# A pre-norm decoder layer: the wide row blocks of three Gram matrices from 12-bit parts

## The chip, the core and the metric

The kernel runs on one core of a Trainium2 chip. The core has five engines with a queue of instructions each: TensorE (PE, matrix multiplication; its weight loads are listed apart as PEld), VectorE (DVE), ScalarE (ACT), GpSimd (POOL) and SyncE (SP, which only issues transfers here). Engines work through their own queues in order and wait for one another through semaphores. The metric is the time of one execution on the device, in microseconds (us); lower is better.

## The reference, cut to what matters

One decoder layer, batch 4, sequence length T = 512, model width D = 512, all in float32: attention, cross-attention and a feed-forward part, each behind a layer norm and added to x.

```python
def attn(x, ...):                       # 16 heads of 128; x is layer-normed
    q = (x @ Wq + bq).reshape(4, 512, 128, 16).transpose(0, 3, 2, 1)   # 128 x T
    k = (x @ Wk + bk).reshape(4, 512, 128, 16).transpose(0, 3, 1, 2)   # T x 128
    v = (x @ Wv + bv).reshape(4, 512, 128, 16).transpose(0, 3, 2, 1)
    att = softmax(q @ k / sqrt(128))    # 128 x 128: over channels, not positions
    return concat_heads(att @ v) @ Wo + bo
x = x + attn(layernorm(x))
x = x + gamma * cross(layernorm(x), ctx, ctx)   # q, k, v cut into 8 heads of 64 x 512
x = x + (silu(h @ w1q.T) * (h @ w3q.T)) @ w2q.T # h = layernorm(x); HID = 1365
```

w1q, w3q and w2q are the ternary-quantised weights, w + (q - w) with q = clip(round(w / s), -1, 1) * s and s the mean of |w|.

The scores of a head are a contraction over the T rows: q k = Wq' (xn' xn) Wk, with xn the normed rows and the bias carried by a column of ones. So xn' xn, a matrix of 512 x 512 called the Gram matrix, serves all heads of a batch. It is symmetric.

## The kernel before

**Stages.** The first batch's attention comes first, with the weights prepared beside it. Then a loop over b = 1 to 3 (L977) does the attention of the second, third and fourth batch, and inside it, as side steps, the cross-attention of the batch before and the quantisation of w1, w3 and w2. The feed-forward part of all batches follows (L1069 on), with the last batch's cross-attention in it.

**Parts.** Most products of attention are not made in float32. A tensor is held as three tiles, h, l and d (class `Tri`; `tri_of`, L187): h is the source times H_OF, rounded to the 12 bits that a one-pass matmul takes (type fp32r), l the source less h, and d = h / S - l, with S = 4096. `products` (L329) sums h h + l l over four row groups in one PSUM bank (L336, L337), copies it to SBUF on ScalarE (L343), sums d d in another bank (L348), and `total` (L358) joins the two on VectorE with the factor 1 + 1/S on the first. A product is then 12 matmuls of one pass for 4 in float32. The parts of the weights lie in DRAM and are loaded again for every batch by SP's queue into an 18-buffer pool; for `o` in the second batch h and l alone are loaded and VectorE makes d (L322, from ol, a tile of ones and oh) in `weights`.

**The Gram matrix** is `gram_upper` (L422). xn lies in SBUF as four tiles xs[g] of 128 rows (on the partitions) x 512 columns. For row block m (0 to 3) only the columns from m * 128 on are made, so the blocks are 512, 384, 256 and 128 wide, each a sum of four float32 matmuls, evicted by ScalarE into G[m] (L420). In the second to fourth batch the order is m = 0, 1, 2, 3; after m = 1, `midway` transposes on TensorE (bank pe, copied to eT by ScalarE) the softmax e of the last group of heads of the batch before. `output` (L548, bank po) then applies that softmax and adds into the four tiles acc on VectorE. `gram_rest` (L451) fills the lower blocks by transposes of upper ones (bank gt, L458) and splits G[0] to G[3] into parts gh, gl, gd.

**The groups of heads.** For each batch and each of four groups of four heads (j): `values_out` (banks pu: x parts by Wo parts, giving u and its parts), `keys_of` (py: G parts by Wk parts, giving y), `output` of the group before, `values_of` (pm: Wv parts by u parts, giving m), and `scores` (bank sc, float32: q by y, then the softmax). x3, the parts of xn, is made by `parts_of`: at the end of the first batch for the second one, and in the last group of a batch for the next, ahead of `values_of`.

**Order.** Each engine runs its instructions in the order in which a scheduler of the compiler put them; that order is fixed when the kernel is built. The side steps are handed out by `tick`, a fixed number per piece of a product. Among them are the row norms of the batch before (`row_norms`: mv_c on VectorE, two transfers through DRAM that GpSimd issues, norm_a and norms, L673 and L676, and then settle on norms, L596), the inputs of cross-attention (qs, kh, kl: L707 to L716), its scores (bank xs, L726 and L727) and its output (bank xo, L770). GpSimd issues the side steps' transfers, the loads of x into acc and the load of the bias bo; its few computations before are casts in the feed-forward part (L138).

**Pools** that the change touches: u3p (12 buffers, parts of u), yp (5, where G and y lie), tp (3, the SBUF copies of PSUM banks).

Of the kernel before, what the change touches and what calls it, by code (L numbers as in the profile page):

```python
# [19 lines left out]
P = 128  # L20
# [19 lines left out]
def decoder_layer_kernel(  # L40
# [25 lines left out]
    def bank(name):  # L66
        return psum.tile([P, 512], F32, tag="bank", name=name)
# [147 lines left out]
    def exact(n, b, j):  # L215
        return b > 0 or j >= FIRST[n]
# [202 lines left out]
    def evict(dst, src):  # L419
        nc.scalar.copy(dst, src)  # L420

    def gram_upper(b, xs, midway=None):  # L422
        pool, tag = (x3p, "x3") if b == 0 else (yp, "y")
        G = [pool.tile([P, D], F32, tag=tag, name=f"G_{b}_{m}") for m in range(KC)]
        pg = {}

        def add(m, g):
            if g == 0:
                pg[m] = bank(f"pg_{b}_{m}")
            nc.tensor.matmul(  # L430
                pg[m][:, : D - m * P],
                lhsT=xs[g][:, ts(m, P)],
                rhs=xs[g][:, m * P :],
                start=(g == 0),
                stop=(g == NG - 1),
            )
            if g == NG - 1:
                evict(G[m][:, m * P :], pg[m][:, : D - m * P])


        if b == 0:
            order = [(m, g) for g in range(NG) for m in range(KC)]
        else:
            order = [(m, g) for m in range(KC) for g in range(NG)]
        for m, g in order:
            add(m, g)
            if midway and (m, g) == (1, NG - 1):
                midway()
        return G

    def gram_rest(b, G):  # L451

# [40 lines left out]
    def values_of(b, j, w, u3, tick):  # L493
        ms = {}

        def done(g, h, d):
            ms[g] = mp.tile([P, D], F32, tag="m", name=f"m_{b}_{j}_{g}")
            total(ms[g], h, d)

        products(f"pm_{b}_{j}", lambda k, g: cols(w[k], g), lambda k: u3[k], done, tick)  # L500
        return ms

    def scores(b, j, w, ys):

        scale = (S if exact("k", b, j) else 1.0) / math.sqrt(DH)
        sc = bank(f"sc_{b}_{j}")
        for g in range(NG):
            for k in range(KC):
                nc.tensor.matmul(  # L509
                    sc[:, ts(g, DH)],  # L510
                    lhsT=w[k][:, ts(g, DH)],
                    rhs=ys[k][:, ts(g, DH)],
                    start=(k == 0),
                    stop=(k == KC - 1),
                )
        nmax = small.tile([P, NG], F32, tag="nmax", name=f"nmax_{b}_{j}")
        mark["nmax"] = nc.vector.reduce_max(
            nmax, sc.rearrange("p (h k) -> p h k", h=NG), axis=AX.X
        ).ins
        nc.vector.tensor_scalar(nmax, nmax, -scale, None, ALU.mult)  # L520
        e = ep.tile([P, GW], F32, name="e")
        den = small.tile([P, NG], F32, tag="den", name=f"den_{b}_{j}")
        for g in range(NG):
            nc.scalar.activation(
                e[:, ts(g, DH)],
                sc[:, ts(g, DH)],
                AF.Exp,
                bias=nmax[:, g : g + 1],
                scale=scale,
                accum_out=den[:, g : g + 1],  # L530
            )
        rden = small.tile([P, NG], F32, tag="rden", name=f"rden_{b}_{j}")
        nc.vector.reciprocal(rden, den)
        for g in range(NG):
            nc.vector.tensor_scalar(
                e[:, ts(g, DH)], e[:, ts(g, DH)], rden[:, g : g + 1], None, ALU.mult
            )
        return e
# [326 lines left out]
    for j in range(HG):  # L865
        us, ys, ms = {}, {}, {}

        def to(tiles, pool, tag, name):
            def done(i, p, d=None):
                tiles[i] = pool.tile([P, 512], F32, tag=tag, name=f"{name}_{i}")  # L870
                if d is None:
                    evict(tiles[i], p)
                else:
                    total(tiles[i], p, d)

            return done

        ticks = [0]

        def third_tick():  # L880
            ticks[0] += 1
            if ticks[0] == 3:
                midway()

        def midway():
            if waiting:
                waiting[2] = turned(*waiting[:3])

        w = first_weights("o", j, first, gates["o"])
        if exact("o", 0, j):  # L890
            w = keep_weights("o", j, w, first, gates["o"])
            products(
                f"pu_0_{j}", lambda c, m: cols(x3[c], m), lambda c: w[c],
                to(us, u3p, "u3", f"u_0_{j}"), lambda: None,
            )
        else:
            products_f32(
                f"pu_0_{j}", lambda c: xs[c], lambda c: w[c], to(us, u3p, "u3", f"u_0_{j}")
            )
            if j == 0:  # L900
                g3 = gram_rest(0, G)
            with tc.issue_after(rows_done):
                keep_weights("o", j, w, first, gates["o"])
        gates["v"] = gate_of(us[3])
        if j == 1:
            biased(accs, bo_bc)
        w = first_weights("k", j, first, gates["k"])
        done = to(ys, yp, "y", f"y_0_{j}")
        if exact("k", 0, j):
            w = keep_weights("k", j, w, first, gates["k"])  # L910
            products(
                f"py_0_{j}", lambda e, m: cols(g3[e], m), lambda e: w[e], done, third_tick
            )
        else:
            products_f32(f"py_0_{j}", lambda e: G[e], lambda e: w[e], done, midway)
            keep_weights("k", j, w, first, gates["k"])
        gates["o"] = gates["k"] = gates["q"] = gate_of(ys[3])
        if waiting:
            output(*waiting)
        w = first_weights("v", j, first, gates["v"])  # L920
        products_f32(f"pm_0_{j}", lambda k: w[k], lambda k: us[k], to(ms, mp, "m", f"m_0_{j}"))
        keep_weights("v", j, w, first, gates["v"])
        w = first_weights("q", j, first, gates["q"])
        if j == HG - 1:
            normed(1, xs, False)
        e = scores(0, j, w, ys)
        keep_weights("q", j, w, first, gates["q"])
        if j == 0:
            bo_bc = bias_rows(0)
            load(gam, gamma.to_broadcast([P, 1]))  # L930
        if j + 1 == FIRST["o"]:
            x3 = parts_of(0, xs)
        if j == HG - 2:
            xs = rows_of(1)
        if j == HG - 1:

            with tc.issue_after(mark["nmax"]):
                x3 = parts_of(1, xs)
        waiting = [0, j, e, ms, accs]
    first_pools.close()  # L940

    inputs_f = {}
# [34 lines left out]
    for b in range(1, B):  # L977
        def midway():
            waiting[2] = turned(*waiting[:3])

        G = gram_upper(b, xs, midway)
        recent[:] = [G[0], G[0]]
        output(*waiting)
        side = Side(
            itertools.chain(row_norms(b - 1, waiting[4]), cross(b - 1, *cpool)),
            NORM_STEPS + CROSS_STEPS,
            TICKS + 6,
        )

        def tick():  # L990
            quant.tick()
            side.tick()

        bo_bc = bias_rows(b)
        g3 = gram_rest(b, G)
        for j in range(HG):
            u3 = values_out(b, j, x3, weights("o", b, j, wp), tick)
            if j > 0:
                waiting[2] = turned(*waiting[:3])
            ys = keys_of(b, j, g3, weights("k", b, j, wp), tick)  # L1000
            if j > 0:
                output(*waiting)
            else:
                accs = accumulators(b, bo_bc)
            if j == HG - 2:
                xs = rows_of(b + 1)
            if j == HG - 1 and b + 1 < B:
                normed(b + 1, xs, False)
                x3 = parts_of(b + 1, xs)
            elif j == HG - 1:  # L1010
                for t in xs:
                    settle(t)
                ffn_0 = prepare_ffn(0, xs)
                for _ in range(NC):
                    next(ffn_0)
            ms = values_of(b, j, weights("v", b, j, wp), u3, tick)
            e = scores(b, j, weights("q", b, j, wp), ys)
            if j == 0:
                biased(accs, bo_bc)
            waiting = [b, j, e, ms, accs]  # L1020
        side.rest()
# [155 lines left out]
```

## Time and profile before

| | us |
|---|---|
| median of 3 runs | 1152.76 (1149.95 to 1154.46) |
| profiled execution, span | 1150.0 |
| TensorE busy | 1140.7 |
| VectorE busy | 818.7 |
| ScalarE busy | 523.5 |
| GpSimd busy | 295.9 |
| third batch: Gram matrix, first matmul to output | 409.21 to 418.39 |

How to read it: the span is the time from the first to the last instruction of one execution; the profiled execution is a single one and stands 2.8 us below the median of the timed runs. Busy times overlap, since engines work side by side. In rows of a timeline the columns are start (us), duration (us), engine, line, operation, out<-in by the program's names, tile shapes and the number of instructions that the row puts together; an idle time before it and what ended it stand in brackets. The mean of the granted TensorE clock is 0.999 of full speed. The DMA engines moved 235 GB/s in the mean, and were busy for 0.8 and more of the time in most slices of the first 800 us.

### The profile page before, as it was taken

How to read it: one execution, taken by the hardware profiler on the slowest of the kernel's cores; microseconds unless marked ns; L12 is line 12 of the kernel's file. 1: busy time of each engine (PE TensorE's matmuls, PEld its weight loads, DVE VectorE, ACT ScalarE, POOL GpSimd, SP SyncE). 2: the span in 40 equal slices, each digit the busy share in tenths (PEclk: the TensorE clock that was granted, in tenths of full speed). 3: DMA queues.
4: the chain of work that ended last, by engine and by line, in shares of the span. 5: the costliest groups of instructions: out<-in, count | busy, mean ns of one | idle time of the engine just before them, and what ended most of it. 6: DMA issues, size and time to landing. Idle time of an engine off the chain costs nothing.

```text
span 1150.0 us, 16662 instructions
## 1 busy us (share of the span) xinstructions
PE 1140.7 (99%) x5310; PEld 858.6 (75%) x5310; DVE 818.7 (71%) x1818; ACT 523.5 (46%) x1071; POOL 295.9 (26%) x534
## 2 busy tenths in 40 slices
PE   9999999999999999999999999999999999999998
PEld 5486585787778767877776787777778877777886
DVE  6857766978788965969696769788857856536242
ACT  4534334354535442644354445445355768534020
POOL 3435433433133232213221422122113212000000
PEclk9999999999999999999999999999999999999999
DMA  9999996998889769988986798799791422122100
GB/s 332 306 344 337 345 314 225 324 319 280 281 281 308 261 201 325 312 272 276 321 291 215 256 334 271 254 330 325 268 304 40 122 79 65 48 73 72 64 1 37
DMA packets 146177, 270.68 MB, mean 235 GB/s; under 512 B 18276, under 2 KB 49300, under 8 KB 146090
## 3 DMA queue, kind: packets, MB, share of 16 engines
q1 hardware_dynamic: 112218, 164.93, 43.4%
q0 software_dynamic: 33872, 104.70, 26.8%
q8 instruction: 42, 0.69, 0.2%
q14 instruction: 45, 0.37, 0.1%
HBM read 206.62 MB, written 62.93 MB: 234 GB/s over the span
## 4 chain that ended last, share of the span: by engine, by line
PE 96%; DMA 2%; DVE 1%; issue 1%; ACT 0%; POOL 0%; SPq 0%; DVEq 0%; POOLq 0%; ACTq 0%
PE h L1084 13%; PE y L1119 7%; PE xo L770 5%; PE xp L126 5%; PE po L548 5%; PE pm L370 5%; PE sc L509 5%; PE pg L430 3%; PE xs L727 3%; PE xs L726 2%; PE pu_2h L336 1%; PE pu_1d L348 1%; PE py_3h L336 1%; PE py_3h L337 1%; PE pu_2h L337 1%; PE py_2h L337 1%
## 5 line engine op out<-in xcount | busy, mean ns | idle before, releaser
L1084 PE MATMUL h<-fxh,t 128*128 128x512 f32 (+1 forms) x352 | 139.6, 397 | 0.0
L1084 PE MATMUL h<-fxl,t 128*128 128x512 f32 (+1 forms) x352 | 137.4, 390 | 0.0
L737 ACT ACTIVATE p<-xs,xnmax 128x512 f32<-128x512 f32 x128 | 87.2, 689 | 84.8 <-PE xp L126 68.2
L731 DVE TENSOR_REDUCE xnmax<-xs 128x1 f32<-128x512 f32 x128 | 83.5, 684 | 19.3 <-PE xs L727 19.3
L1084 PEld LDWEIGHTS h<-fxh,t 128*128 128x128 f32 (+1 forms) x352 | 65.0, 185 | 15.4 <-issue 1.1
L1084 PEld LDWEIGHTS h<-fxl,t 128*128 128x128 f32 (+1 forms) x352 | 65.0, 185 | 14.7 <-issue 0.2
L1119 PE MATMUL y<-t,gh 128*128 128x512 f32 (+1 forms) x176 | 69.3, 394 | 0.0
L1119 PE MATMUL y<-t,gl 128*128 128x512 f32 (+1 forms) x176 | 68.8, 391 | 0.0
L129 ACT COPY pt<-xp 128x512 f32<-128x512 f32 x96 | 54.1, 595 | 31.0 <-PE xp L126 31.0
L126 PE MATMUL xp<-ident,p 128*128 128x128 f32 x512 | 66.5, 273 | 0.0
L126 PEld LDWEIGHTS xp<-ident,p 128*128 128x128 f32 x512 | 59.3, 140 | 9.4 <-issue 2.4
L770 PE MATMUL xo<-pt,vals 128*64 128x512 f32 x256 | 61.5, 599 | 0.0
L1097 DVE SCALAR_TENSOR_TENSOR gf<-h,scales_w,sl 128x512 f32<-128x512 f32 (+1 forms) x44 | 32.9, 747 | 39.8 <-PE h L1084 36.4
L749 DVE TENSOR_SCALAR p<-p,xrden 128x512 f32<-128x512 f32 x128 | 56.7, 486 | 2.9
L548 PE MATMUL po<-m,eT 128*128 128x512 f32 x128 | 57.6, 593 | 0.0
L1093 ACT ACTIVATE sl<-h,scales_w 128x512 f32<-128x512 f32 (+1 forms) x44 | 30.1, 688 | 58.7 <-PE h L1084 58.5
L689 POOL DMA_DIRECT2D xd<-x_a x64 | 33.8, 532 | 88.6 <-DVE qs L710 64.5
L370 PE MATMUL pm<-u,v_raw 128*128 128x512 f32 x128 | 55.6, 592 | 0.0
L727 PE MATMUL xs<-kl,qs 128*128 128x512 f32 x128 | 50.1, 391 | 0.5 <-DVE kl L714 0.5
L138 POOL CAST gh<-gf 128x512 fp32r<-128x512 f32 (+1 forms) x24 | 15.8, 660 | 134.9 <-DVE gf L1097 119.7
L726 PE MATMUL xs<-kh,qs 128*128 128x512 f32 x128 | 50.1, 392 | 0.0
L139 DVE TENSOR_TENSOR gl<-gf,gh 128x512 fp32r<-128x512 f32 (+1 forms) x44 | 30.4, 690 | 26.3 <-POOL gh L138 19.3
(313 smaller groups left out, 2897.6 us busy)
## 6 DMA issues: line engine op xcount, KB each, us to landing
oh<-kept_oh SPq DMA_DIRECT2D x48, 256.0 KB, 5.9
ol<-kept_ol SPq DMA_DIRECT2D x48, 256.0 KB, 6.2
kh<-kept_kh SPq DMA_DIRECT2D x48, 256.0 KB, 5.2
kl<-kept_kl SPq DMA_DIRECT2D x48, 256.0 KB, 5.9
vh<-kept_vh SPq DMA_DIRECT2D x48, 256.0 KB, 6.6
vl<-kept_vl SPq DMA_DIRECT2D x48, 256.0 KB, 6.9
q<-kept_q SPq DMA_DIRECT2D x48, 256.0 KB, 6.6
od<-kept_od SPq DMA_DIRECT2D x44, 256.0 KB, 6.8
```

Of the source, the lines that this page charges most:

```text
L126: nc.tensor.transpose(pt[:, ts(k, P)], src[:, ts(k, P)], ident)
L370: nc.tensor.matmul(p, lhsT=lhs(k)[:, ts(i, P)], rhs=rhs(k), start=(k == 0), stop=(k == 3))
L509: nc.tensor.matmul(sc[:, ts(g, DH)], lhsT=w[k][:, ts(g, DH)], rhs=ys[k][:, ts(g, DH)], start=(k == 0), stop=(k == KC - 1),)
L548: nc.tensor.matmul(po, lhsT=eT[:, g, :], rhs=ms[g], start=True, stop=True)
L726: nc.tensor.matmul(sc, lhsT=q[:, ts(m, P)], rhs=kh, start=True, stop=False)
L727: nc.tensor.matmul(sc, lhsT=q[:, ts(m, P)], rhs=kl, start=False, stop=True)
L731: nc.vector.reduce_max(nmax[:, i : i + 1], scs[i], axis=AX.X)
L737: nc.scalar.activation(p, scs[i], AF.Exp, bias=nmax[:, i : i + 1], scale=xscale, accum_out=den[:, i : i + 1],)
L749: nc.vector.tensor_scalar(ps[i], ps[i], rden[:, i : i + 1], None, ALU.mult)
L770: nc.tensor.matmul(po[half, :], lhsT=vals[c][:, l, half], rhs=pt[j][:, l, :], start=(l == 0), stop=(l == NC - 1),)
L1084: nc.tensor.matmul(ph[:r, :], lhsT=t[:, block(i, k)], rhs=fxT[j][:, k, :], start=(k == 0 and j == 0), stop=(k == KC - 1 and j == 1),)
L1119: nc.tensor.matmul(py, lhsT=g[i][j][:r, ts(c, P)], rhs=t2[:r, i, :], start=(i == 0 and j == 0), stop=(i == NHC - 1 and j == 1),)
```

## The change

For the second to fourth batch `gram_upper` makes the narrow blocks (m = 2 and 3) first, in float32 as before, with the factor 1/S at the eviction. The wide blocks (m = 0 and 1) are made from the parts x3 that the batch's pu products use anyway: h by a scaled copy of h (h / S, the new tiles xs_b_g) and l by l into banks pgh, then `midway`, two copies on ScalarE (tiles pgt), d by d into banks pgd, and on VectorE G = (1 + 1/S) * pgt - pgd. So the whole of G is 1/S of what it was; `scores` multiplies its scale by S in these batches. `scaled_rows` makes the four scaled tiles on GpSimd, in buffers of u3p: behind the first batch's loop for the second batch, and in the last group of heads, between `values_of` and `scores`, for the next one. The first batch is as before. In the changed kernel later lines move down: the softmax's po from L548 to L586, for instance, xs from L726 and L727 to L764 and L765; the scaling is L485, the new matmuls L457, L460 and L472, the copies L467 and the joining L475.

```diff
--- before.py
+++ after.py
@@ -419,7 +419,7 @@
     def evict(dst, src):
         nc.scalar.copy(dst, src)
 
-    def gram_upper(b, xs, midway=None):
+    def gram_upper(b, xs, midway=None, x3=None, scaled=None):
         pool, tag = (x3p, "x3") if b == 0 else (yp, "y")
         G = [pool.tile([P, D], F32, tag=tag, name=f"G_{b}_{m}") for m in range(KC)]
         pg = {}
@@ -435,18 +435,56 @@
                 stop=(g == NG - 1),
             )
             if g == NG - 1:
-                evict(G[m][:, m * P :], pg[m][:, : D - m * P])
+                if b == 0:
+                    evict(G[m][:, m * P :], pg[m][:, : D - m * P])
+                else:
+                    nc.scalar.mul(G[m][:, m * P :], pg[m][:, : D - m * P], 1.0 / S)
 
 
         if b == 0:
-            order = [(m, g) for g in range(NG) for m in range(KC)]
-        else:
-            order = [(m, g) for m in range(KC) for g in range(NG)]
-        for m, g in order:
-            add(m, g)
-            if midway and (m, g) == (1, NG - 1):
-                midway()
+            for g in range(NG):
+                for m in range(KC):
+                    add(m, g)
+            return G
+        for m in range(2, KC):
+            for g in range(NG):
+                add(m, g)
+        upper = (0, 1)
+        ph = {m: bank(f"pgh_{b}_{m}")[:, : D - m * P] for m in upper}
+        for m in upper:
+            for g in range(NG):
+                a, c = x3[g], slice(m * P, D)
+                nc.tensor.matmul(
+                    ph[m], lhsT=a.h[:, ts(m, P)], rhs=scaled[g][:, c], start=(g == 0), stop=False
+                )
+                nc.tensor.matmul(
+                    ph[m], lhsT=a.l[:, ts(m, P)], rhs=a.l[:, c], start=False, stop=(g == NG - 1)
+                )
+        midway()
+        hs = {}
+        for m in upper:
+            hs[m] = tp.tile([P, 512], F32, tag="t", name=f"pgt_{b}_{m}")[:, : D - m * P]
+            nc.scalar.copy(hs[m], ph[m])
+        for m in upper:
+            pd = bank(f"pgd_{b}_{m}")[:, : D - m * P]
+            for g in range(NG):
+                a = x3[g]
+                nc.tensor.matmul(
+                    pd, lhsT=a.d[:, ts(m, P)], rhs=a.d[:, m * P :], start=(g == 0), stop=(g == NG - 1)
+                )
+            nc.vector.scalar_tensor_tensor(
+                G[m][:, m * P :], hs[m], 1.0 + 1.0 / S, pd, ALU.mult, ALU.subtract
+            )
         return G
+
+    def scaled_rows(b, x3):
+
+        tiles = []
+        for g in range(NG):
+            t = u3p.tile([P, D], F32R, tag="u3", name=f"xs_{b}_{g}")
+            nc.gpsimd.tensor_scalar(t, x3[g].h.bitcast(F32), 1.0 / S, None, ALU.mult)
+            tiles.append(t)
+        return tiles
 
     def gram_rest(b, G):
 
@@ -502,7 +540,7 @@
 
     def scores(b, j, w, ys):
 
-        scale = (S if exact("k", b, j) else 1.0) / math.sqrt(DH)
+        scale = (S if exact("k", b, j) else 1.0) * (S if b > 0 else 1.0) / math.sqrt(DH)
         sc = bank(f"sc_{b}_{j}")
         for g in range(NG):
             for k in range(KC):
@@ -937,6 +975,7 @@
             with tc.issue_after(mark["nmax"]):
                 x3 = parts_of(1, xs)
         waiting = [0, j, e, ms, accs]
+    scaled = scaled_rows(1, x3)
     first_pools.close()
 
     inputs_f = {}
@@ -978,7 +1017,7 @@
         def midway():
             waiting[2] = turned(*waiting[:3])
 
-        G = gram_upper(b, xs, midway)
+        G = gram_upper(b, xs, midway, x3, scaled)
         recent[:] = [G[0], G[0]]
         output(*waiting)
         side = Side(
@@ -1014,6 +1053,8 @@
                 for _ in range(NC):
                     next(ffn_0)
             ms = values_of(b, j, weights("v", b, j, wp), u3, tick)
+            if j == HG - 1 and b + 1 < B:
+                scaled = scaled_rows(b + 1, x3)
             e = scores(b, j, weights("q", b, j, wp), ys)
             if j == 0:
                 biased(accs, bo_bc)
```

## The prediction, made before the changed kernel ran

> **What bounds the kernel now.** I read the page's engine shares and its chain of waits first, then the timelines of TensorE and of its weight loads around a Gram matrix, then VectorE and GpSimd at the same places.
>
> ```profile
> PE 1140.7 (99%) x5310; PEld 858.6 (75%) x5310; DVE 818.7 (71%) x1818; ACT 523.5 (46%) x1071; POOL 295.9 (26%) x534
> ...
> PE 96%; DMA 2%; DVE 1%; issue 1%; ACT 0%; POOL 0%; SPq 0%; DVEq 0%; POOLq 0%; ACTq 0%
> ```
>
> TensorE (PE) has work in 99% of the span and the chain runs through it for 96%. So TensorE time that goes is gained, and each wait that appears on TensorE is lost; all else counts only through such a wait. Third batch, TensorE's Gram matrix, then sixteen one-pass matmuls of py (first and next row):
>
> ```profile
> 409.21 6.28 PE L430 MATMUL pg<-xn 128*128 128x512 f32 x16
> 415.33 0.60 PE L126 MATMUL pe<-ident,e 128*128 128x128 f32 x4
> 415.77 2.78 PE L430 MATMUL pg<-xn 128*128 128x256 f32 x16
> 418.39 3.60 PE L548 MATMUL po<-m,eT 128*128 128x512 f32 x8
> ...
> 409.75 0.19 PEld L430 LDWEIGHTS pg<-xn 128*128 128x128 f32 x1 [0.24 <-issue]
> 410.18 0.19 PEld L430 LDWEIGHTS pg<-xn 128*128 128x128 f32 x1 [0.24 <-issue]
> ...
> 433.42 0.39 PE L336 MATMUL py_0h<-kh,gh 128*128 128x512 f32 x1
> ...
> 437.07 1.19 PE L348 MATMUL py_0d<-kd,gd 128*128 128x512 f32 x4
> ```
>
> Durations overlap, so starts count. A float32 matmul is two records 0.43 us apart (410.18 - 409.75): 0.86 us for 512 columns. A one-pass matmul of 512 columns takes (437.07 - 433.42) / 16 = 0.228. The wide blocks hold TensorE for 415.33 - 409.21 = 6.12 us, 3.43 of it for 512 columns, so 2.69 for 384; the narrow ones for 418.39 - 415.77 = 2.62.
>
> **The matmuls.** In each of three batches 8 wide float32 matmuls (6.12 us) give way to 24 one-pass ones. The 12 of 512 columns cost 12 x 0.228 = 2.74. No row has one of 384 columns: not under half a record of that width (2.69 / 8 / 2 = 0.168), not over 0.228. I take 0.228 x 0.336 / 0.43 = 0.178, by the ratio of the float32 rows: 2.14. So 6.12 - 4.88 = 1.24 us saved per batch (0.6 to 1.4), 3.7 in all. The narrow blocks are the same matmuls, placed first.
>
> **ScalarE.** Two copies out of PSUM go (0.59 and 0.48 us) and two of the same sizes come (L467); the narrow evictions get a factor. Nothing is added, but the copies of the wide blocks end later.
>
> **VectorE, second batch.** Two results per batch are added (L475): 0.69 us as for od below, and some 0.53 for 384 columns. What matters is what stands behind them: L475 needs the last d matmul, and this queue keeps its order. Before, od, made from ol and oh in this batch only, stood between the x parts and po:
>
> ```profile
> 195.57 0.68 DVE L189 TENSOR_TENSOR xl<-xn,xh 128x512 fp32r<-128x512 f32 x1
> ...
> 199.31 1.41 DVE L322 SCALAR_TENSOR_TENSOR od<-ol,one,oh 128x512 fp32r<-128x512 f32 x2
> ...
> 204.47 0.75 DVE L322 SCALAR_TENSOR_TENSOR od<-ol,one,oh 128x512 fp32r<-128x512 f32 x1
> ...
> 206.91 1.98 PE L348 MATMUL pu_0d<-od,xd 128*128 128x512 f32 x8
> ```
>
> VectorE has no gap from 195.57 on; od was complete at 205.2, 1.7 us before TensorE used it. In the built order of the changed kernel the four od stand behind both L475, four acc and all eight gl and gd. From the end of G_0's last d matmul: 0.25 us until VectorE starts, 0.6 + 0.5 for L475, 4 x 0.65 for acc, 8 x 0.605 (their spacing in a row) for gl and gd, 0.1 for two small ones, 0.5 of waiting for gh_2 (two evictions and two gh behind gt): od_0 starts after 9.4 and ends after 10.2. TensorE from the same moment: the last matmul of G_1 0.17, po 3.43, gt 0.4, sixteen pu_0h 3.64, two more gt 0.2: it wants od_0 after 7.9. It waits 2.3 us; the next od follow 0.66 apart, as fast as TensorE takes them. Later in this stage the 0.87 us that pm_0d waited for vd shrinks, since transfers go on meanwhile: I credit 0.4. Net 1.9 lost (0 if VectorE and ScalarE catch up, 2.5 without the credit).
>
> **GpSimd.** Twelve multiplications of 128x512 are new. The nearest rows are its casts, 0.62 us alone, and this one:
>
> ```profile
> 964.22 0.75 DVE L710 SCALAR_TENSOR_TENSOR qs<-xd,norms,qs 64x512 fp32r<-64x512 f32 x1
> ...
> 964.32 1.13 POOL L138 CAST gh<-gf 128x512 fp32r<-128x512 f32 x1 [7.28 <-DVE gf L1097]
> ```
>
> Beside a VectorE operation that reads two tensors from SBUF the cast ended only 0.48 us after that one: 0.5 longer. [...] By the row second-batch Gram comes out even, by a wait to the end of the run 2.7 us longer, as in the second case below.
>
> In the third and fourth batch the x parts are made some 8 us before Gram needs them (last xd at 401.32, Gram at 409.21 and its narrow part first), so 4 x 1.13 = 4.5 us is hidden; without that cover it would all be a stall. In the second batch nothing covers it. xs_1 to xs_3 stand in GpSimd's queue behind loads that waited until 190.54 for the scores and ended at 192.17, and xs_2 needs xh_2, which ScalarE finished at 195.05. With 1.13 each: xs_1 at 193.3, xs_2 at 196.2, xs_3 at 197.4. TensorE starts at 190.08, is through the narrow blocks at 192.70 and the first two row groups at 194.5, waits for the softmax (VectorE, 195.0) and for xs_2, and ends at 199.2, against 199.16 before. So here the 1.24 saved is eaten by idling: 0 (-0.3 with multiplications of 0.62).
>
> **Queues.** SP's order does not change. GpSimd's loads of acc wait for st_c, which VectorE now does behind gd; that moves about 1 MB later. norm_a and norms also move, see the third case. The changed softmax scale costs nothing.
>
> **Sum.** Second batch 0 + 1.9 = +1.9; third and fourth -1.24 each; +0.6 as half of the 1.2 us by which VectorE, held up by GpSimd at 397 to 403, may hand pt late to xo in the third batch. That is 0.0: span 1150.0, as before. The runs' median is 1152.76, 2.8 over the profiled span, so 1152.8, and I say 1153. Own range of this case: 1150 to 1156.
>
> **The rivals.**
>
> 1. *Full gain.* No stall in the second batch: -3.7, 1149. For it: VectorE's order is all that delays od. Against it: both queues are written down and the sum above misses by 2 us. Chance 0.12.
>
> 2. *GpSimd held to the end of a run of VectorE operations.* xs_2 starts at 195.1, but xl_2, xd_2, xl_3 and xd_3 follow without a gap until 198.1, so it ends at 198.55, xs_3 at 199.2; with 3.1 us of matmuls behind xs_2, po starts at 201.75 and not 199.16: +2.6. With od +1.9, the other batches -2.5 and pt late in full, 1.2: +3.2, 1156. For it: the cast above made next to no progress beside qs. Against: no row shows two such operations in a row beside GpSimd. Chance 0.20.
>
> 3. *The row norms come late (the other side).* Third batch, before:
>
> ```profile
> 432.17 0.55 POOL L673 DMA_DIRECT2D norm_a<-mv_c  x1 [0.34 <-DVE mv_c L672]
> ...
> 439.67 1.40 POOL L676 DMA_DIRECT2D norms<-norm_a  x2 [5.01 <-DMA norm_a<-mv_c]
> ...
> 445.08 0.16 DVE L596 TENSOR_TENSOR norms<-norms,one 128x1 f32<-128x1 f32 x1
> ```
>
> mv_c to norms took 13.2 us through two transfers, at a DMA share of 0.99. Now mv_c's copy stands behind y_0_0 and y_0_1, which ended at 441.85: some 440.9 with TensorE 1.2 earlier, so norms at 454.1. VectorE and ScalarE stand still at it; qs, kh, two m and kl follow until 458.1. TensorE's first xs, at 462.4 before, comes at 461.1: 3 us to spare, 8 before. In the fourth batch norms at 664.39 becomes 670, kl 674, xs 677: 3 us again. If each of the transfers takes 3 us longer than before, 6 - 3 = 3 us are lost per batch, 6 in all: 1159. It decides once mv_c to norms exceeds 16 us. Against: acc's loads, moved later, leave room for the weights just before. Chance 0.26.
>
> That the change doesn't do what it says is left 0.01: with h, l and d as built, (1 + 1/S)(h h/S + l l) - d d is G/S, and the softmax multiplies by S.
>
> **How the numbers follow.** The first reading has 0.41. Half a per cent is 5.8 us, about what a measurement of this kernel can tell from no change. Faster by that needs more than the whole saving: 0.07, for the full gain with the waits for kd (1.04 us) and vd (0.87) gone too, which makes 3.7 + 1.9 = 5.6, and something more. Slower by that is most of the third rival and the tail of the second: 0.25. Within: 0.68. The range reaches from the full gain, 1148.5, to the third rival with transfers that take 3.5 us longer each instead of 3, which adds 2: 1161.
>
> **What would show it.** In the profile of the changed kernel: 24 one-pass matmuls of L457, L460 and L472 per batch, 4.9 us without a gap in the third and fourth; TensorE idle before L457 in the second, released by POOL; idle before pu_0d there, released by DVE od L322, about 2 us; L485 at 0.62 to 1.13 us, and longer beside runs of VectorE if the second rival holds; mv_c to norms, and idle before L764 xs, for the third. I am wrong if od isn't waited for, if the 384-column matmuls cost as much as those of 512, or if a wait far from Gram carries the difference.

## The result and the profile after

The changed kernel takes 1159.70 us in the median of four runs (1158.46 to 1160.71), the kernel before 1152.44 (1149.95 to 1154.46). The ratio, taken over all executions, is 1.0067, with a 95% interval of 1.0051 to 1.0083: slower by 5.9 to 9.6 us, 7.7 by the ratio itself. Below, a difference that stands beside a ratio is that ratio's and not that of the two medians. The profiled execution has a span of 1158.9 us against 1150.0.

The engine shares and the chain of waits of the changed kernel, the two lines that were read first before:

```profile
PE 1142.9 (99%) x5334; PEld 865.1 (75%) x5334; DVE 823.5 (71%) x1824; ACT 523.8 (45%) x1071; POOL 315.6 (27%) x546
...
PE 87%; DMA 5%; DVE 4%; issue 2%; ACT 1%; POOL 1%; SPq 0%; DVEq 0%; POOLq 0%; ACTq 0%
```

TensorE's share of the chain fell from 96% to 87%; transfers now hold 5% of it and VectorE 4%. TensorE's busy time did not fall by the 3.7 us that were forecast, but rose by 2.2: the three Gram matrices have 2.6 us of work less, one stretch at half speed (below) has 3.5 more, and smaller pieces add 1.3, 0.7 of it ahead of the second batch. The other 6.7 of the 8.9 us that the span grew are waits. The list of TensorE's waits (us in total, times, longest):

```profile
PE py_0d L348 <- DMA kd<-kept_kd: 3.3, 3, 1.3
PE pu_1d L348 <- DMA od<-kept_od: 2.3, 4, 1.1
PE pu_0d L348 <- DVE od L322: 1.7, 1, 1.7
PE pgh L457 <- POOL xs L485: 1.4, 2, 1.0
```

The first was 1.0 before and the second 0.7; the last two are new. Lining up TensorE's matmuls of the two profiled executions, one by one, gives where the 8.9 us arise (the shift of the changed kernel against the one before at the end of each stretch, and by how much it changed in that stretch; beside it what the prediction had there):

| stretch | shift at its end | measured | predicted |
|---|---|---|---|
| up to the second batch's Gram matrix | 0.41 | +0.41 | 0 |
| that Gram matrix, to po | 1.36 | +0.95 | 0 |
| po to pu_0d | 3.22 | +1.86 | +2.3 |
| to the third Gram matrix | 3.68 | +0.46 | +0.2 (-0.4 for vd, +0.6 for pt) |
| third Gram matrix | 2.54 | -1.14 | -1.24 |
| to the fourth | 3.17 | +0.63 | 0 |
| fourth Gram matrix | 2.25 | -0.92 | -1.24 |
| first py of the fourth batch | 9.05 | +6.80 | 0 |
| the rest | 8.93 | -0.12 | 0 |

The +0.63 on the way to the fourth Gram matrix is what is left of two larger changes: the waits for kd that the kernel before has at 438 to 440 us are spared (the shift falls from 2.4 to 0.8), and new waits for od bring it to 3.1.

The one-pass matmuls do what was said of them. Third batch, TensorE's timeline:

```profile
412.89 2.88 PE L430 MATMUL pg<-xn 128*128 128x256 f32 x16
415.53 0.47 PE L457 MATMUL pgh<-xs,xh 128*128 128x512 f32 x1
...
418.87 0.60 PE L126 MATMUL pe<-ident,e 128*128 128x128 f32 x4
419.22 1.87 PE L472 MATMUL pgd<-xd 128*128 128x512 f32 x8
420.93 3.60 PE L586 MATMUL po<-m,eT 128*128 128x512 f32 x8
```

The 24 take 418.87 - 415.53 = 3.34 and 420.93 - 419.22 = 1.71, so 5.05 us for the 6.12 of the float32 ones (4.88 were forecast). The whole Gram matrix with its transposes takes 8.04 us; it was 9.18.

Most of the loss is in a place that holds no changed instruction, the first py of the fourth batch:

```profile
658.30 0.61 PE L348 MATMUL py_0d<-kd,gd 128*128 128x512 f32 x2
660.25 0.73 PE L348 MATMUL py_0d<-kd,gd 128*128 128x512 f32 x2 [1.34 <-DMA kd<-kept_kd]
662.12 1.22 PE L348 MATMUL py_0d<-kd,gd 128*128 128x512 f32 x2 [1.13 <-DMA kd<-kept_kd]
664.17 1.22 PE L348 MATMUL py_0d<-kd,gd 128*128 128x512 f32 x2 [0.82 <-DMA kd<-kept_kd]
665.19 0.63 PE L336 MATMUL py_0h<-kh,gh 128*128 128x512 f32 x1
```

TensorE waits three times for kd, 3.3 us in all. And look at the last line: a one-pass matmul of 512 columns, 0.39 us long in most rows of this record, is 0.63 long; the next starts 0.43 behind it and not 0.228. The busy time by stretches says why (the column behind POOL is the granted clock, then the share of the transfer engines and GB/s):

```profile
660.00:662.00 2.00, 0.73 (x2) 0.30 (x2) 0.46 (x1) 0.77 (x2) 0.00 (x0) 1.00 1.04 383
662.00:664.00 2.00, 1.22 (x2) 0.50 (x2) 0.00 (x0) 0.00 (x0) 0.00 (x0) 0.50 1.05 391
664.00:666.00 2.00, 1.83 (x4) 1.49 (x5) 1.00 (x2) 0.00 (x0) 0.00 (x0) 0.50 0.93 341
666.00:668.00 2.00, 2.00 (x6) 1.57 (x5) 1.21 (x6) 0.00 (x0) 1.04 (x2) 0.50 0.40 94
668.00:670.00 2.00, 2.00 (x8) 1.59 (x8) 0.00 (x0) 0.00 (x0) 0.04 (x1) 0.79 1.00 355
```

From 662.0 to 668.8 TensorE is granted half its clock. That costs half of 6.8, 3.4 us, and with the waits 6.7 of the 6.8 in the table. It is no accident of the execution that was profiled: the mean granted clock of the four was 0.996, 0.997, 0.997 and 0.997, and 0.003 of 1150 us is 3.5; the kernel before stands at 0.999 to 1.000.

Why kd is late, by the list of transfers issued between 640 and 665 us (size, then the median time from issue to landing):

```profile
acc<-in_x_dram POOLq DMA_DIRECT2D x4, 256.0 KB, 6.8
kd<-kept_kd SPq DMA_DIRECT2D x4, 256.0 KB, 10.1
```

and by the same list for the kernel before, between 638 and 663:

```profile
acc<-in_x_dram POOLq DMA_DIRECT2D x4, 256.0 KB, 4.9
kd<-kept_kd SPq DMA_DIRECT2D x4, 256.0 KB, 6.2
```

SP issues kd just as early against TensorE as before (7.6 us behind the start of pu_0h in both, 651.01 - 643.43 and 648.76 - 641.18), but it takes 3.9 us longer to land. In the five microseconds behind 645.3 the transfer engines move 130 GB/s, at a share of 0.40; at the same point of the kernel before it was 252, at 0.78. GpSimd issued the four loads of acc at 643.1 to 647.7 before, ahead of kd. Now they leave at 650.4 to 659.4, in among kd and vh, since each waits for the st_c (the statistics of the row norms) that reads its buffer, and VectorE has those behind gd. The first and the last of the four, before:

```profile
643.08 0.54 POOL L849 DMA_DIRECT2D acc<-in_x_dram  x1 [0.52 <-DMA x_a<-acc]
...
647.67 0.57 POOL L849 DMA_DIRECT2D acc<-in_x_dram  x1 [1.12 <-DVE st_c L95]
```

and now:

```profile
650.41 1.19 POOL L887 DMA_DIRECT2D acc<-in_x_dram  x2
...
659.37 0.54 POOL L887 DMA_DIRECT2D acc<-in_x_dram  x1 [0.67 <-DVE st_c L95]
```

### The profile page after: what moved, and what is told of

Same layout as the page of the kernel before. It is cut to its first block, busy times and chain, and to the rows that moved or that the text cites. A ratio compares the mean times of both kernels' runs of the same rounds, so it can differ in the third digit from the quotient of the medians.

```text
span 1158.9 us, 16756 instructions
## 1 busy us (share of the span) xinstructions
PE 1142.9 (99%) x5334; PEld 865.1 (75%) x5334; DVE 823.5 (71%) x1824; ACT 523.8 (45%) x1071; POOL 315.6 (27%) x546
## 4 chain that ended last, share of the span: by engine, by line
PE 87%; DMA 5%; DVE 4%; issue 2%; ACT 1%; POOL 1%; SPq 0%; DVEq 0%; POOLq 0%; ACTq 0%
PE h L1125 10%; PE y L1160 7%; PE pm L370 5%; PE xo L808 5%; PE xp L126 5%; PE po L586 4%; PE sc L547 4%; PE xs L765 2%; PE xs L764 2%; DMA od<-kept_od 2%; PE pu_2h L336 1%; PE py_3h L336 1%; PE py_3h L337 1%; PE pu_2h L337 1%; PE py_2h L336 1%
## 5 line engine op out<-in xcount | busy, mean ns | idle before, releaser
L727 POOL DMA_DIRECT2D xd<-x_a x64 | 33.9, 533 | 95.8 <-DVE qs L748 66.7
L586 PE MATMUL po<-m,eT 128*128 128x512 f32 x128 | 57.6, 592 | 0.0
L765 PE MATMUL xs<-kl,qs 128*128 128x512 f32 x128 | 50.1, 391 | 0.1
L764 PE MATMUL xs<-kh,qs 128*128 128x512 f32 x128 | 50.1, 391 | 0.0
```

The costliest lines, as they stand in the source:

```text
L586: nc.tensor.matmul(po, lhsT=eT[:, g, :], rhs=ms[g], start=True, stop=True)
L764: nc.tensor.matmul(sc, lhsT=q[:, ts(m, P)], rhs=kh, start=True, stop=False)
L765: nc.tensor.matmul(sc, lhsT=q[:, ts(m, P)], rhs=kl, start=False, stop=True)
```

## The experiments

Theory A is that account: a changed order on VectorE moves 1 MB of loads onto the weights' transfers, and the waits that follow, 3.3 us in the fourth batch, go with 6.8 us at half clock. There are two rivals: the loss is GpSimd's and VectorE's in the second batch (B), or the shift from the second batch moves other work onto kd (C). Each run stands beside executions of the kernel before that were timed along with it; their median lies between 1151.5 and 1152.2.

**One batch at a time.** In the changed kernel `gram_upper` makes parts only for the batches named, the scale of the softmax following:

```diff
-        if b == 0:
+        if b not in (3,):     # (1,) and (2,) in the two other runs
```

> Only the fourth batch's Gram matrix is made of parts; the second and third are float32 as before. Theory A (row norms' statistics and with them the loads of acc moved behind gd, so that they share the transfers with kd; TensorE waits for kd and then runs at half clock): -0.9 for the matmuls, +3.3 waiting, +3.4 for half a clock during 6.8 us, so +5.8: about 1158. Theory B (the fourth batch's stall is an accident of one execution, the loss belongs to GpSimd and VectorE in the second batch): -0.9, about 1151.5, and no wait for kd. Theory C (the shift of some 3 us from the second batch put the quantisation's transfers on top of kd): also -0.9, since nothing is shifted here.

> Only the second batch's Gram matrix is made of parts. Theory A: +0.9 for a Gram matrix that waits for the scaled rows and +1.9 for od, so about +3: 1155.5, no half clock. Theory B: this is where the whole loss is, +7: 1159.5. Theory C: +3 and in the fourth batch the wait for kd all the same, 1159 to 1162.

> Only the third batch's Gram matrix is made of parts. Theory A: -1.1 for the matmuls and up to +2 for weights that land later than before (acc's loads beside them), between 1151.3 and 1153.5. If row norms that come late hold up the cross-attention (the third rival of the prediction): +3, 1155.5, with TensorE idle before its first xs.

Fourth batch alone: 1156.65 against 1151.51, ratio 1.0039 (1.0024 to 1.0053), +4.5 us. Second alone: 1155.78, 1.0031 (1.0019 to 1.0044), +3.6. Third alone: 1152.17, 1.0005 (0.9995 to 1.0014), +0.6. They add up to 8.7, against 7.7 for all three by its ratio. The first excludes B and C as the whole cause: nothing is shifted ahead of the fourth batch there, and still

```profile
PE py_0d L348 <- DMA kd<-kept_kd: 4.1, 3, 2.6
```

Of the 4.1, 2.6 are one wait at 657.6, and the half clock, from 659.8 on, lasts 3.4 us and not 6.8, which fits a time below the 1158 expected. In the second batch's run TensorE waits for od (1.7) and the scaled rows (1.4), as theory A has it; not as it has it, it also waits 1.9 in the feed-forward part. That is the profiled execution, with a mean clock of 0.999 and at 1158.8 the longest of the six; four of the others have a clock of 1.000, so the +3.6 does not hang on the clock.

**The order without the change.** In the kernel before, all float32, the statistics of the third and fourth batch's row norms are put where the changed kernel has them:

```diff
-            tri_of(tri, G[m])
+            mark["gd"] = tri_of(tri, G[m])
...
-            moments(mv[:, g, :], accs[g], f"c_{b}_{g}")
+            with tc.issue_after(mark["gd"]) if b + 1 < B else nullcontext():
+                moments(mv[:, g, :], accs[g], f"c_{b}_{g}")
```

> The kernel before, all Gram matrices in float32; in the third and fourth batch the statistics of the row norms (st_c) are put behind the last gd on VectorE, as they stand in the changed kernel, and nothing else is edited. Theory A: the loads of acc come late and TensorE waits for kd in the fourth batch by some 3 us, followed by a stretch at half clock: +3 to +7, 1155.5 to 1159.5. Theory B and C: 1152.4, no wait for kd beyond the 1.0 us of before.

1155.37 us, ratio 1.0035 (1.0021 to 1.0049): +4.0 with not one matmul changed. Its waits:

```profile
PE py_0d L348 <- DMA kd<-kept_kd: 1.6, 2, 1.2
PE pu_1d L348 <- DMA od<-kept_od: 1.3, 2, 0.7
...
PE pm_0d L348 <- DMA vd<-kept_vd: 0.7, 1, 0.7
```

Lined up with the kernel before, TensorE falls back by 0.6 and 0.4 at kd of the third and fourth batch, by 0.6 and 0.6 at od, and by 1.2 at vd, 3.4 of this execution's 3.8. In the fourth batch vh lands after 8.1 us (7.0 before), vl after 9.0 (7.6) and kd after 6.6 (6.2). So the expected 3 us of waiting for kd there, with half a clock behind it, did not come in this execution, whose mean clock is 1.000. The order by itself costs the 4.0 us, with the loads of acc later and no other change. But the place is not the same: in this execution it is kd, od and vd, by the amounts above. That the stall of the fourth batch in particular is theirs rests on the next run, in which they leave early again and it goes.

**The order mended in the change.** The four `moments` stand directly behind `output(*waiting)`, ahead of `gram_rest`:

```diff
         output(*waiting)
+        mvs[b - 1] = stats_of(b - 1, waiting[4])
...
```

> The changed kernel with the statistics of the row norms (st_c) put right behind the output of the batch before, ahead of the last gl and gd on VectorE, so that the loads of acc go out early again. Theory A: the wait for kd in the fourth batch (3.3) and the half clock behind it (3.4) go; in the second batch the four st_c now stand ahead of od, which costs up to 2.5: 1159.7 - 6.7 + 2.5 = 1155.5, between 1153 and 1156. Rival (kd is late because the whole stage has more transfers at that time, whoever issues them): no gain, 1159 to 1162.

1156.80 us (1152.17 before), ratio 1.0047 (1.0032 to 1.0062). In time this is outside the expected 1153 to 1156, and a small gain that the intervals don't tell from none; in the profile both halves of the expectation are there: the wait for kd is gone from the list, kd lands after 5.8 us, and

```profile
PE pu_0d L348 <- DVE od L322: 4.1, 1, 4.1
```

od, behind four st_c now, is waited for in the second batch, and half a clock follows from 211.5 to 218.3. Lined up with the kernel before, this run is 9.0 us behind at 227 us, 7.5 at 254, and 4.9 at its end: past the second batch the changed Gram matrices gain 2.6. The price of the second batch had been set too low, by that clock.

**od ahead of the Gram matrix.** The first Wo weights of the second batch are asked for before `gram_upper`, so that VectorE makes od in a gap of 3.5 us ahead of the softmax:

```diff
+        if b == 1:
+            recent[:] = [xs[0], xs[0]]
+            o_first = weights("o", 1, 0, wp)
         G = gram_upper(b, xs, midway, x3, scaled)
...
```

> The changed kernel with the d parts of the first Wo group of the second batch (od) made before the Gram matrix, in VectorE's gap ahead of the softmax, not behind gd. Theory A: the wait before pu_0d (1.7) goes, what follows it in the second batch too (0.2 to 0.7): 1159.7 - 2 = 1157.7. Rival (the scaled rows on GpSimd set the pace there, so that the wait moves to gd or to another tile): 1159.7.

1155.58 us, ratio 1.0031 (1.0017 to 1.0046). The wait for od made on VectorE is gone, and the kernel is faster than the changed one by 4.1 us by the ratios, where 2 were expected. The ten executions differ more than any others here, 1151.7 to 1159.8: the profiled one waits for kd for 1.8 us with the clock at 1.000 and takes 1151.71, the two longest have 0.995 and 0.996. The same instructions, in the same order, cost the clock or not; what decides between these executions was not shown.

**Parts earlier, and ScalarE for GpSimd.** Two edits for the scaled rows of the second batch:

```diff
-            with tc.issue_after(mark["nmax"]):
-                x3 = parts_of(1, xs)
+            x3 = parts_of(1, xs)
```

> The changed kernel with the parts xl and xd for the second batch no longer held behind the softmax's maximum of the last group of the first batch, so that VectorE makes them in its gap and GpSimd can scale the rows earlier. Theory A: the two waits for the scaled rows (1.4) go and Gram in the second batch takes 8.1 instead of 10.0: 1159.7 - 1.9 = 1157.8, if the softmax behind them is not late by more than 1. Rival (GpSimd is slowed by VectorE in any case and the rows are late again): 1159 to 1160.

```diff
-            nc.gpsimd.tensor_scalar(t, x3[g].h.bitcast(F32), 1.0 / S, None, ALU.mult)
+            nc.scalar.mul(t, x3[g].h.bitcast(F32), 1.0 / S)
```

> The changed kernel with the twelve scaled rows made by ScalarE (some 0.63 each by its own casts of the same size) in place of GpSimd (1.5 to 2.5). If GpSimd's length is what makes Gram wait in the second batch: the waits for the scaled rows (1.4) go and VectorE's operations beside them get shorter, 1159.7 - 1.5 to -2.5 = 1157.2 to 1158.2. Rival (ScalarE gets late with xh, eT and pgt instead): 1159 to 1161. The wait for kd in the fourth batch stays in both.

1157.68 us (1.0047, 1.0031 to 1.0064) and 1157.22 (1.0049, 1.0028 to 1.0070). Both times are as theory A expected, but their intervals don't tell them from the changed kernel's, and neither reason held. The waits for the scaled rows do go, but the next thing is late at once. With the parts earlier, the Gram matrix does not take the 8.1 us expected but 11.5 (190.40 to 201.94), in an execution whose mean clock is 0.998:

```profile
PE pe L126 <- DVE e L573: 2.2, 1, 2.2
```

and with ScalarE, the same wait, shorter:

```profile
PE pe L126 <- DVE e L573: 1.4, 1, 1.4
```

The softmax e of `midway`, not GpSimd, is the limit of the second batch's Gram matrix once the rows are in time: it takes 9.6 us with ScalarE (190.77 to 200.39), 10.0 with GpSimd, 9.1 for float32.

**Both orders mended.** od ahead of the Gram matrix, and the early statistics for the third and fourth batch only:

> The changed kernel with both orders mended: od of the second batch ahead of its Gram matrix, and st_c of the third and fourth batch right behind the output, ahead of the last gl and gd. Theory A: no wait before pu_0d, no wait for kd, no half clock in the fourth batch; left are +0.9 in the second batch's Gram matrix, up to +1 behind it, and -1.1 and -0.9 in the others, with some of the before kernel's waits for od and kd gone too: 1150 to 1152.5 against 1152 before. Rival (waits for weights come from the transfers' total and only move): 1154 to 1156.

1150.58 us against 1151.67, ratio 0.9994 (0.9986 to 1.0003). This is as expected: no time is left of the loss. TensorE's longest waits in it:

```profile
PE pgh L457 <- POOL xs L485: 1.3, 2, 1.0
PE pu_1d L348 <- DMA od<-kept_od: 1.3, 1, 1.3
```

kd lands after 6.1 us and is not waited for; the profiled execution has a mean clock of 1.000. The rival, that the transfers' total decides and waits only move, falls.

**Two batches, and the control.** The same early statistics, with parts in the third and fourth batch only, and with no parts at all:

> Parts in the third and fourth batch only (the second in float32 as before), with st_c of these two right behind the output. Theory A: -1.1 and -0.9 for the matmuls, -0.5 to -1.5 for waits for od and kd of the kernel before that this order spares: 1148.5 to 1150, a ratio of 0.997 to 0.9985. Rival: the transfers' total decides, 1151 to 1153.

> The control: float32 Gram matrices everywhere, with st_c of the third and fourth batch right behind the output, as in the run with two batches. Theory A: the order before was already early, so at most the spared waits, -0.5 to -1.5: 1150.5 to 1152, and the difference to the run with two batches, some 2, is what the one-pass matmuls are worth. Rival (the gain of that run is the order alone): the same time as that run.

1151.37 us (ratio 0.9999, 0.9989 to 1.0009) and 1151.07 (0.9997, 0.9988 to 1.0006). This is a miss: the third and fourth Gram matrix take 8.04 and 12.05 us to po, in the control 9.17 and 12.95 (the fourth has xo's matmuls inside), so 2.0 are saved, but the run is not faster than its control. In the profiled execution the gain goes back in waits that lie far from it, 2.0 us ahead of xt_f in the feed-forward part (0.5 in the control) and 1.5 for od (0.8). Over eleven executions what cancels the 2 us isn't shown; it stays open.

**All of it.** Both orders mended and ScalarE in GpSimd's place:

> The run with both orders mended, and the scaled rows made by ScalarE in place of GpSimd. Theory A (GpSimd's 1.5 to 2 us for a scaled row is what holds Gram in the second batch, 1.3 of waits in that run): 0.4 to 1.3 less than that run, 1149.3 to 1150.2, a ratio of 0.998 to 0.9988. Rival (the softmax that ScalarE and VectorE make for the output is what comes next, as in the earlier run with ScalarE, where TensorE waited 1.4 for e): the same as that run, 1150.6, or 1 more.

1151.32 us against 1151.94, ratio 0.9994 (0.9985 to 1.0002): the same as with GpSimd. The rival held, with 1.5 us of waiting for e where 1.3 for the scaled rows had been. No version beats the kernel before by more than its interval, so that no run shows the matmuls' saving as time.

## Why the prediction was right and wrong, by its steps

The range (1148.5 to 1161) held the time, and that is luck: its upper part was there for row norms that come late, and those cost nothing. The forecast case, no change at 1153, was wrong by 6.7 us; the time is the third rival's (1159), by another way than its own; and slower by more than half a per cent, which came, had been given 0.25. By a sign that the prediction itself had named, it was wrong: "if a wait far from Gram carries the difference".

- *The matmuls* were right: 1.14 and 0.92 us saved in the third and fourth batch for 1.24 each. The eight of 384 columns in pgh (417.45 to 418.87) take 0.178 each, as was put. That the saving can't be told in the time of a kernel with both orders mended was not foreseen.
- *The queues* are the step that failed. It said of acc's loads, held by st_c behind gd, that this "moves about 1 MB later", and gave it no price; the third rival even counted it as an argument against itself, that they "leave room for the weights just before". They took the room of the weights. The runs with the fourth batch alone (+4.5) and with the order alone (+4.0) show it; with the order mended the wait for kd is gone.
- *The third rival* had the right kind of cause, statistics that come later on VectorE, and the wrong victim. mv_c was done at 442.83 where 440.9 was forecast and norms at 455.28 (454.1), but TensorE's first xs of the third batch started at 463.14, with no wait. The 3 us to spare were enough, as mv_c to norms took 12.5 us and not 16.
- *Half a clock* was in no case. It made 3.4 of the 8.9 us. The prediction priced waits one for one; here 3.3 us of waiting cost 6.7.
- *od* was right in kind and order, 1.7 us of waiting for 2.3, and the 1.86 that this stretch lost. The 0.4 credited for vd did not come (0.8 waited for, 0.87 before).
- *pt late*, 0.6 of the sum, did not come: from 250.7 us to the third Gram matrix the shift stays at 3.6 to 3.8, and the list of TensorE's waits has none between 395 and 414 us.
- *GpSimd* was mis-sized. All twelve multiplications, shortest, median and longest in ns, in the changed kernel:

```profile
L485 POOL TENSOR_SCALAR xs<-xh x12: 1484/1577/2494, 186.7 to 620.0; 128x512 fp32r<-128x512 f32 x12
```

  The nearest row, a cast, had 0.62 to 1.13. So Gram in the second batch was not even but 0.95 longer; the second rival's 2.6 was too much. With ScalarE (the last run) the same rows take

```profile
L485 ACT ACTIVATE xs<-xh x12: 632/644/664, 186.8 to 619.4; 128x512 fp32r<-128x512 f32 x12
```

  The longest, 2.49, lay beside VectorE's xl and xd, and VectorE paid too: the xd beside the row at 405.16 took 1.04 us where others take 0.69. But the first, at 186.71, took 1.50 with VectorE idle for all but its first 0.3 us, and the median of the twelve, 1.58, lies 0.08 above it, so the overlap with VectorE is the smaller part of the error. Moving the work to ScalarE gained no time that the runs can tell.

## What to carry to other kernels

A shorter product changes when everything around it becomes ready, and the scheduler answers with another order on engines that aren't the bound. For each instruction that moves, ask which buffer it frees and which transfer that starts, and lay those transfers beside the ones that TensorE needs next; 1 MB per batch that left later, in the fourth by some 5 to 9 us, cost here 4.0 us by itself, more than the forecast saving of 3.7. And price TensorE's waits with what they may do to the clock, not only with their length: here 2.4 us of them within 3.4 us came ahead of 6.8 us at half clock.

## What the runs showed of the hardware

Leaving out the first and the last 10 us of a kernel, the granted clock falls to half in the changed kernel at 662.0 us, for 6.83, within the second of three waits of TensorE in a row (1.34, 1.13 and 0.82); in the run with the order mended at 211.5, for 6.8, within a wait of 4.1; and with the fourth batch alone at 659.8, for 3.4, within one of 2.6. It did not fall behind a wait of 1.67 in the changed kernel (at 208.5), nor in the kernel before, where the longest was 0.87. In two profiled executions with a mean clock of 1.000 the longest waits were 2.0 (parts in two batches) and 1.7 (od ahead of the Gram matrix); 3.4 us at half clock would have lowered that mean by 0.0015. So the length of a single wait does not decide in these executions.

In the 3.41 us ahead of the fall at 662.0 (half as long as the 6.83 behind it) TensorE was busy for 1.05; in 3.41 us with the wait of 1.67 in them (208.04 to 211.45) it was busy for 1.74. In the first 3.41 us at half clock it was busy for 2.48, and half clock went on; in the next for all 3.41, and full clock followed. The author's estimate from these figures is that waits close together count together, as 1.34 and 1.02 of the 1.13 do ahead of 662.0. What sets the clock, and from how much idle time on it falls, was not shown.
